# A two-layer graph network on one core: another order of the first and last stages, and their small operations on other engines

## The chip, the core and the metric

The kernel runs on one core of a Trainium2 chip. The core has a matrix engine (TensorE, PE in the profile), three engines for element-wise work (VectorE or DVE, ScalarE or ACT, GpSimd or POOL), and SyncE (SP), whose queue here issues nearly all transfers. Each engine works through its own list of instructions strictly in order; semaphores make one engine wait for another. The metric is the device time of one execution in microseconds (us); lower is better.

## What is computed

128 graphs, each with 128 nodes of 512 features (x) and a weighted adjacency matrix of 128x128 (adj). Everything is fp32.

```python
# layer 0
h = relu(layernorm(x))
# hypergraph conv, twice: H = (adj != 0), w = adj's first row
#   xw = x @ W.T ; m = Be * (H.T @ xw) ; out = Dn * (H @ m) + b
#   Dn = 1 / (H @ w), Be = 1 / column sums of H
h1 = layernorm(relu(hypergraph_conv(h, adj, W1, b1)), gamma, beta)   # 512 -> 1024
x = x + hypergraph_conv(h1, adj, W2, b2) + h                         # 1024 -> 512
# layer 1
h = relu(layernorm(x))
agg = (adj @ h) / max(rowsum(adj), 1e-6)
x = x + relu(concat([h, agg]) @ W.T)
```

gamma and beta of the inner layer norm are folded into the second weight matrix: its rows are scaled by gamma (scale_w2), and beta times it is a constant row (beta_row, summed on TensorE over eight parts, beta_out).

## The kernel before, in words

**Products in three parts.** TensorE multiplies fp32 at full precision slowly and a shorter format (fp32r) fast. So both factors of every large product are split in a high part h and a low part l, and a third combination d corrects the sum: product() (line 413) makes h times h and l times l in one PSUM bank (pm) and d times d in another (pd). The three weight matrices, each in two halves (w1, w2, w3, class Half), are split once at the start: high() on ScalarE, low() on VectorE, and rest(), which makes d, on VectorE or GpSimd (l - h, one instruction of 1024 columns) or, without an engine, on TensorE with a unit matrix and two ScalarE copies.

**One graph, in stages.** Each stage is a small function with the graph's number. x_sums, x_spread, scales, x_norm are the first layer norm; incidence (VectorE, from adjb, a copy of adj laid out in 32x32 blocks) and node_matrix make the 128x128 node operator S and Dn; conv1_nodes applies it, conv1_high/low/rest split the result, conv1_weights(g, half) multiplies with a half of w1; conv1_main (ScalarE) and conv1_out (VectorE) bring pm and pd into R, conv1_bias adds b1. inner_sums, inner_spread, inner_norm normalise R. For the transpose R goes to DRAM and comes back in blocks: inner_out, inner_in (four transfers), inner_turn; inner_high/low/rest split it, conv2_weights multiplies with w2, conv2_main, conv2_weights_out, conv2_bias give G, conv2_nodes and conv2_out add the result to x. residual (GpSimd) adds h and b2 to x. Layer 1 goes the same way: layer1_sums to layer1_norm, layer1_trip_out and layer1_trip_in through DRAM, layer1_turn, high, low, rest, then layer1_mean (the half of w3 for the mean, split again by layer1_mean_high/low/rest), layer1_self (the other half), aggregate with the transposed mean matrix (mean_operator, mean_out, mean_in, mean_transpose, mean_rest), layer1_self_main, layer1_self_out, finish with the store.

**The order is written out by hand.** Under manual_schedule the instructions of each engine stand in the order in which the stages are called. step(s) (line 694) is the steady loop; it works on the graphs from s - 4 to s + 3 at once. A stage that has been called for a graph is not done again (the set done, line 107), and calls for graphs that do not exist do nothing. So head() (line 761) may do stages of the first graphs early, and the loop leaves them out; tail() (line 986) does what the loop has left for the last five graphs, which it calls a to e (123 to 127). For the last graph tail() transposes on TensorE (layer1_now, turned_now, line 535) in place of the way through DRAM.

**Queues and buffers.** A stage's engine argument says where it runs: conv1_bias, conv2_bias, inner_low, layer1_low and layer1_mean_low run on GpSimd, in pieces of 256 columns, unless nc.vector is given. x_t has six buffers and adjb two, but R, G/H3 (tag A), H0 (tag B) and the landing tiles of the round trips have one, so that a stage can have to wait until the last reader of the graph before is through. PSUM has six banks for products (w) and two for node products (n).

**Fillers.** fill(columns) puts matmuls of a constant (line 94) ahead of the next product, into its bank; their result is overwritten. head() has ten of them and tail() three, 9600 columns in all.

Of the kernel before, what the change touches and what calls it, by code (L numbers as in the profile page):

```python
# [24 lines left out]
def gnn_kernel(  # L25
# [31 lines left out]
    nc = tc.nc  # L57
# [305 lines left out]
    @stage  # L363
    def x_spread(g):
        spread((1, g), X[g], H0[g], D)
# [395 lines left out]
    def head():  # L761
        copy(eps_root, eps, AF.Sqrt)
        load_x(0)
        load_adjb(2)
        for half in range(2):
            for i in range(2):
                load_w1(half, i)
        load_affine()
        unit()
        load_adjb(0, nc.scalar)  # L770
        load_adjb(1)
        load_x(1)
        x_sums(0)
        load_adj(0)
        x_spread(0)
        scales(0, 1)
        for half in range(2):
            load_w2(half)
        load_bias(b2_bc, b2)
        x_norm(0)  # L780
        w1[0].high(0)
        w1[0].high(1)
        load_x(2)
        incidence(0)
        w1[0].low(0)
        fill(2944)
        node_matrix(0)
        conv1_nodes(0)
        w1[0].low(1)
        w1[1].high(0)  # L790
        conv1_high(0)
        w1[1].high(1)
        w1[0].rest(0, nc.vector)
        load_bias(b1_bc, b1)
        conv1_low(0)
        conv1_rest(0)
        x_sums(1, "A")
        x_spread(1)
        node_scale(0)
        w1[0].rest(1, nc.vector)  # L800
        scales(1, 1)
        w1[1].low(1)
        fill(512)
        x_norm(1)
        incidence(1)
        w1[1].low(0)
        conv1_weights(0, 0)
        conv1_main(0, 0)
        beta_row(0)
        scale_w2(0, nc.scalar)  # L810
        node_matrix(1)
        beta_row(1)
        scale_w2(1, nc.scalar)
        w1[1].rest(0, nc.vector)
        w1[1].rest(1, nc.vector)
        w2[0].high(0)
        conv1_nodes(1)
        conv1_high(1, True)
        conv1_weights(0, 1)
        conv1_low(1)  # L820
        conv1_rest(1)
        beta_row(2)
        beta_row(3)
        conv1_main(0, 1)
        conv1_out(0, 0)
        scale_w2(2, nc.vector)
        load_adjb(3)
        scale_w2(3, nc.vector)
        conv1_weights(1, 0)
        conv1_bias(0, 0, nc.vector)  # L830
        w2[0].high(1)
        conv1_out(0, 1)
        conv1_bias(0, 1, nc.vector)
        beta_row(4)
        load_w3(1)
        load_w3(0)
        beta_row(5)
        beta_row(6)
        node_scale(1)
        residual(0)  # L840
        beta_row(7)
        inner_sums(0)
        conv1_weights(1, 1)
        w2[0].low(1)
        inner_spread(0)
        scale_w2(5, nc.vector)
        scale_w2(4, nc.vector)
        scales(0, 2)
        scale_w2(6, nc.vector)
        x_sums(2)  # L850
        scale_w2(7, nc.vector)
        w2[0].low(0)
        incidence(2)
        fill(256)
        inner_norm(0)
        inner_out(0)
        x_spread(2)
        scales(2, 1)
        w2[1].high(0)
        w2[1].low(0)  # L860
        node_matrix(2)
        x_norm(2)
        node_scale(2)
        w2[1].high(1)
        load_adjb(4)
        fill(384)
        conv1_nodes(2)
        conv1_main(1, 0)
        conv1_main(1, 1)
        conv1_high(2)  # L870
        w2[0].rest(1)
        conv1_low(2)
        conv1_rest(2)
        beta_out()
        inner_in(0)
        inner_turn(0)
        residual(1)
        conv1_out(1, 0)
        w3[0].high(0)
        fill(512)  # L880
        load_x(3)
        conv1_out(1, 1)
        w2[1].low(1)
        load_x(4)
        conv1_bias(1, 0, nc.vector)
        inner_high(0)
        conv1_weights(2, 0)
        conv1_bias(1, 1, nc.vector)
        conv1_weights(2, 1)
        inner_low(0, nc.vector)  # L890
        w2[0].rest(0)
        inner_sums(1)
        inner_spread(1)
        x_sums(3)
# [273 lines left out]
```

## Time and profile before

| | |
|---|---|
| three runs | 2497.18, 2497.54, 2499.67 us (median 2497.54) |
| span of the profiled execution, first to last instruction | 2496.5 us |
| mean granted clock of TensorE | 0.999 |
| TensorE, share of the span busy | 99% |
| DMA, share of its 16 engines busy, mean of the 40 slices 1 / 2 / 20 / 40 | 0.6 / 0.3 / 0.4 / 0.2 |
| first matmul of the kernel's own work | 9.23 us |
| last matmul starts | 2491.05 us |
| longest waits of TensorE up to 110 us | third part nd 2.8 (two times), w2 by DMA 2.5, G 1.8 (two times) |

How to read the lines that follow: a row of the timeline gives start, length, engine, line, operation, output<-inputs, shape and count, and in brackets how long the engine was idle before it and what it waited for. Names are those of the program with buffer numbers left out: ps_s is a node matrix's bank, pz and py are node products, rm/rd the two banks of conv1_weights, gm/gd of conv2_weights, bm/bd of layer1_mean, am/ad of layer1_self, pc the beta row. L94 is a filler. A group's length is from the start of its first to the modelled end of its last instruction; because matmuls are pipelined, the distance between two starts is the better measure of work. Rows of windows give start:end, length, busy time of each engine with its number of instructions, the granted clock, the share of the DMA engines that was busy, and GB/s.

### The profile page before, as it was taken

To read this page: it belongs to the slowest core of one execution; us is meant where nothing else is said; L and a number is where in the kernel's file an instruction comes from. 1 tells how busy PE (TensorE), PEld (TensorE's weight loads), DVE (VectorE), ACT (ScalarE), POOL (GpSimd) and SP (SyncE) were. 2 spreads that over 40 slices of the span, in tenths; PEclk is the share of its full clock that TensorE was granted. 3 is DMA by queue.
4 is the path that set the end of the run, shared out by engine and by line. 5 is a ranking of instruction groups with operands and counts; after the bars stand their busy time and mean duration, and the time that the engine had idled before them with its cause. 6 is when DMAs were issued, how large, how long until landed. Compare 5 with 4: busy or idle time off the path is not lost.

```text
span 2496.5 us, 41112 instructions
## 1 busy us (share of the span) xinstructions
PE 2473.9 (99%) x11220; PEld 2008.3 (80%) x11220; DVE 2003.6 (80%) x4913; ACT 1941.1 (78%) x4122; POOL 1701.1 (68%) x2269
## 2 busy tenths in 40 slices
PE   8999999999999999999999999999999999999998
PEld 5688888888888888888888888888888888888886
DVE  7888887888888788888888888888888888888886
ACT  6788778778877877887787788778778877877784
POOL 2476777677667767776776777677677767767770
PEclk9999999999999999999999999999999999999999
DMA  6333443443344344334434433443443344344432
GB/s 176 108 121 120 131 125 120 128 132 121 118 132 126 120 128 131 120 119 126 133 120 128 130 119 121 129 130 120 128 128 122 120 128 132 121 125 130 122 113 87
DMA packets 408951, 311.35 MB, mean 125 GB/s; under 512 B 176656, under 2 KB 339984, under 8 KB 408720
## 3 DMA queue, kind: packets, MB, share of 16 engines
q1 hardware_dynamic: 407888, 308.66, 40.2%
q8 instruction: 88, 1.44, 0.3%
q14 instruction: 143, 1.17, 0.2%
q10 hardware_dynamic: 576, 0.07, 0.0%
q0 software_dynamic: 256, 0.01, 0.0%
HBM read 166.21 MB, written 142.34 MB: 124 GB/s over the span
## 4 chain that ended last, share of the span: by engine, by line
PE 96%; ACT 1%; DVE 1%; DMA 1%; issue 0%; SPq 0%; POOL 0%; DVEq 0%; ACTq 0%
PE rm L422 18%; PE gm L422 18%; PE bm L422 9%; PE rd L427 9%; PE gd L427 9%; PE am L422 9%; PE bd L427 5%; PE ad L427 5%; PE pz L380 4%; PE py L595 4%; PE am L677 2%; PE ad L677 1%; PE ps_s L342 1%; DMA w11r<-in_w1t_dram 0%; ACT junk L266 0%
## 5 line engine op out<-in xcount | busy, mean ns | idle before, releaser
L80 POOL TENSOR_TENSOR g<-g,c 128x256 f32<-128x256 f32 x248 | 178.6, 743 | 634.4 <-DVE g L586 634.4
L80 POOL TENSOR_TENSOR r<-r,b_bc 128x256 f32<-128x256 f32 x496 | 358.1, 743 | 46.4 <-DVE r L447 36.0
L80 POOL TENSOR_TENSOR nl<-nt,nh 128x256 fp32r<-128x256 f32 x500 | 354.6, 741 | 30.3 <-ACT nh L504 30.3
L80 POOL TENSOR_TENSOR x_t<-x_t,b_bc 128x256 f32<-128x256 f32 x256 | 240.6, 959 | 15.3 <-DMA b_bc<-in_b_dram 15.3
L261 ACT ACTIVATE h<-x_t 128x512 f32<-128x512 f32 x256 | 160.0, 625 | 105.3 <-DVE x_t L599 102.9
L671 ACT ACTIVATE o<-am 128x512 f32<-128x512 f32 x128 | 76.5, 598 | 207.4 <-PE am L677 207.4
L80 POOL TENSOR_TENSOR hl<-ht,hh 128x256 fp32r<-128x256 f32 x248 | 231.7, 955 | 2.3 <-ACT hh L504 2.2
L80 POOL TENSOR_TENSOR x_t<-x_t,h 128x256 f32<-128x256 f32 x256 | 181.2, 726 | 45.0 <-ACT h L277 45.0
L277 ACT ACTIVATE h<-x_t,st 128x512 f32<-128x512 f32 x255 | 205.0, 804 | 1.4 <-DVE st L273 1.3
L447 DVE SCALAR_TENSOR_TENSOR r<-rd,dinv,r 128x512 f32<-128x512 f32 x256 | 190.6, 745 | 17.2 <-PE rd L427 2.9
L650 DVE TENSOR_TENSOR gb_t<-bd,gb_t 128x512 f32<-128x512 f32 x128 | 88.6, 692 | 140.4 <-ACT gb_t L646 136.7
L599 DVE SCALAR_TENSOR_TENSOR x_t<-py,dinv,x_t 128x512 f32<-128x512 f32 x128 | 96.1, 750 | 118.5 <-PE py L595 118.5
L266 ACT ACTIVATE h<-x_t,st 128x512 f32<-128x512 f32 x256 | 183.7, 717 | 4.3
L380 PEld LDWEIGHTS pz<-s,h 128*128 128x128 f32 x1024 | 134.3, 192 | 63.5 <-ACT s L344 42.9
L80 POOL TENSOR_TENSOR bl<-gb_t,bh 128x256 fp32r<-128x256 f32 x248 | 179.1, 745 | 0.0
L442 ACT ACTIVATE r<-rm,dinv 128x512 f32<-128x512 f32 x256 | 173.3, 677 | 1.2 <-PE rm L422 1.2
L586 DVE TENSOR_TENSOR g<-gd,g 128x512 f32<-128x512 f32 x128 | 88.5, 692 | 94.6 <-PE gd L427 89.2
L483 DVE STREAM_TRANSPOSE nt<-nb 128x1024 f32<-128x1024 f32 x128 | 157.7, 1232 | 3.8 <-DMA nb<-n_scratch 3.7
L277 ACT ACTIVATE r<-r,st 128x1024 f32<-128x1024 f32 x128 | 157.8, 1233 | 0.9 <-DVE st L273 0.9
L688 DVE SCALAR_TENSOR_TENSOR o<-o,x_t 128x512 f32<-128x512 f32 x128 | 154.5, 1207 | 4.2
L513 DVE SCALAR_TENSOR_TENSOR nd<-nh,nl 128x1024 fp32r<-128x1024 f32 x128 | 155.9, 1218 | 0.0
L422 PE MATMUL rm<-w11h,z 128*128 128x512 f32 x512 | 151.4, 417 | 0.0
(161 smaller groups left out, 7228.2 us busy)
## 6 DMA issues: line engine op xcount, KB each, us to landing
n_scratch<-r SPq DMA_DIRECT2D x128, 512.0 KB, 2.7
nb<-n_scratch SPq DMA_DIRECT2D x512, 128.0 KB, 2.8
x_t<-in_x_dram SPq DMA_DIRECT2D x128, 256.0 KB, 3.1
out_dram<-o SPq DMA_DIRECT2D x128, 256.0 KB, 2.3
h_scratch<-h SPq DMA_DIRECT2D x127, 256.0 KB, 2.0
hb<-h_scratch SPq DMA_DIRECT2D x508, 64.0 KB, 2.0
adj_t<-in_adj_dram SPq DMA_DIRECT2D x128, 64.0 KB, 1.9
an_scratch<-adj_t SPq DMA_DIRECT2D x128, 64.0 KB, 1.7
```

Source lines behind the costliest of these rows:

```text
L80: eng.tensor_tensor(dst[:, s], a[:, s], b[:, s], op)
L261: copy(junk, src, func, accum_out=t[:, 0:1])
L266: copy(junk, src, AF.Square, bias=t[:, 1:2], accum_out=t[:, 2:3])
L277: copy(dst, src, func, bias=t[:, 5:6], scale=t[:, 4:5])
L380: nc.tensor.matmul(z[:, k * P : (k + 1) * P], H0[g][:, k * P : (k + 1) * P], S[g], start=True, stop=True)
L422: nc.tensor.matmul(pm, left[i](k), right(i, k), start=(i == 0 and k == 0), stop=(i == 1 and k == kk - 1))
L427: nc.tensor.matmul(pd, left[2](k), right(2, k), start=(k == 0), stop=(k == kk - 1), skip_group_check=True)
L442: copy(R[g][:, HALVES[half]], PY.pop((g, half)), AF.Copy, scale=DN[g][:, 1:2])
L447: nc.vector.scalar_tensor_tensor(r, PR.pop((g, half)), dn[:, 0:1], r, MUL, ADD)
L483: nc.vector.transpose(nt.rearrange("p k (i b) -> p k i b", b=B), t.rearrange("p i k a -> p k i a"))
L513: nc.vector.scalar_tensor_tensor(t, h, 2.0**-12, low, MUL, SUB)
L688: nc.vector.scalar_tensor_tensor(o, o, 0.0, X.pop(g), MAX, ADD)
```

## The change

head() and tail() get another order; step() and all stages stay as they are. The same stages are done for the same graphs in head() and tail(), with the same number of matmuls on TensorE apart from the fillers. Besides the order:

- fillers: of ten in head() two of 640 columns each remain; the three in tail() are gone; together 1280 columns in place of 9600
- third parts: w1[0].rest(0), w2[1].rest(1) and w3[0].rest(0) go from VectorE to GpSimd; of the five on TensorE w3[1].rest(0), w3[1].rest(1), w3[0].rest(1) and both of w2[0] stay
- bias of conv1: (0, 0), (1, 0), (1, 1), (2, 0), (2, 1) and (127, 0) go from VectorE to GpSimd
- scalings of w2: parts 0, 1, 2, 5, 6 on ScalarE, 3 and 4 on GpSimd, 7 on VectorE (before: 0 and 1 on ScalarE, the rest on VectorE)
- low parts: layer1_low(0), layer1_low(125), layer1_mean_low(124) and (125) from VectorE to GpSimd, inner_low(127) from GpSimd to VectorE
- loads: x(1) and x(0) come first, adjb(0) on ScalarE's queue ahead of its first instruction, b2 and b1 ahead of the second half of w2, adjb(2), adj(0) and w3 later
- graph 1's first sums come ahead of graph 0's, and the square root of eps behind both

The diff, with the old bodies (printed above) cut:

```diff
     def head():
...
+        load_x(1)
+        load_adjb(0, nc.scalar)
+        x_sums(1, "A")
+        load_x(0)
+        x_sums(0)
+        copy(eps_root, eps, AF.Sqrt)
+        load_adjb(1)
+        load_w1(0, 0)
+        x_spread(1)
+        x_spread(0)
+        load_w1(0, 1)
+        incidence(0)
+        node_matrix(0)
+        unit()
+        scales(1, 1)
+        fill(640)
+        scales(0, 1)
+        load_w1(1, 0)
+        load_w1(1, 1)
+        incidence(1)
+        load_w2(0)
+        w1[0].high(0)
+        x_norm(0)
+        w1[0].high(1)
+        load_x(2)
+        load_bias(b2_bc, b2)
+        conv1_nodes(0)
+        node_matrix(1)
+        w1[0].low(0)
+        conv1_high(0)
+        load_affine()
+        load_bias(b1_bc, b1)
+        w1[1].high(0)
+        w1[0].low(1)
+        w1[0].rest(1, nc.vector)
+        w1[1].high(1)
+        node_scale(0)
+        conv1_low(0)
+        x_norm(1)
+        w1[0].rest(0, nc.gpsimd)
+        conv1_rest(0)
+        w1[1].low(1)
+        fill(640)
+        conv1_weights(0, 0)
+        load_w2(1)
+        conv1_nodes(1)
+        beta_row(0)
+        w1[1].low(0)
+        w1[1].rest(1, nc.vector)
+        w1[1].rest(0, nc.vector)
+        load_adjb(2)
+        conv1_main(0, 0)
+        beta_row(1)
+        x_sums(2)
+        conv1_high(1, True)
+        scale_w2(0, nc.scalar)
+        conv1_low(1)
+        conv1_weights(0, 1)
+        beta_row(2)
+        conv1_out(0, 0)
+        scale_w2(1, nc.scalar)
+        conv1_main(0, 1)
+        beta_row(3)
+        x_spread(2)
+        w2[0].high(0)
+        conv1_rest(1)
+        conv1_weights(1, 0)
+        conv1_out(0, 1)
+        beta_row(4)
+        residual(0)
+        conv1_bias(0, 0)
+        conv1_bias(0, 1, nc.vector)
+        inner_sums(0)
+        scale_w2(3, nc.gpsimd)
+        inner_spread(0)
+        scales(0, 2)
+        scale_w2(2, nc.scalar)
+        scale_w2(4, nc.gpsimd)
+        beta_row(5)
+        inner_norm(0)
+        load_w3(0)
+        incidence(2)
+        beta_row(6)
+        w2[0].high(1)
+        node_scale(1)
+        scale_w2(5, nc.scalar)
+        w2[1].high(0)
+        beta_row(7)
+        node_matrix(2)
+        w2[0].low(1)
+        scales(2, 1)
+        inner_out(0)
+        conv1_weights(1, 1)
+        x_norm(2)
+        scale_w2(6, nc.scalar)
+        w2[0].low(0)
+        scale_w2(7, nc.vector)
+        load_adjb(3)
+        load_x(3)
+        beta_out()
+        conv1_main(1, 0)
+        conv1_out(1, 0)
+        conv1_nodes(2)
+        conv1_main(1, 1)
+        conv1_out(1, 1)
+        w2[1].high(1)
+        conv1_high(2)
+        incidence(3)
+        conv1_low(2)
+        conv1_rest(2)
+        inner_in(0)
+        residual(2)
+        x_sums(3)
+        inner_turn(0)
+        w2[1].low(0)
+        w2[1].low(1)
+        conv1_bias(1, 0)
+        conv1_bias(1, 1)
+        w2[0].rest(0)
+        w2[0].rest(1)
+        inner_sums(1)
+        load_w3(1)
+        residual(1)
+        inner_spread(1)
+        load_adj(0)
+        conv1_weights(2, 0)
+        load_adjb(5)
+        scales(1, 2)
+        conv1_weights(2, 1)
+        node_scale(2)
+        w2[1].rest(1, nc.gpsimd)
+        inner_high(0)
+        inner_low(0, nc.vector)
+        x_spread(3)
+        scales(3, 1)
+        node_matrix(3)
+        inner_rest(0)
+        w2[1].rest(0, nc.vector)
+        conv2_weights(0)
+        inner_norm(1)
+        inner_out(1)
+        load_x(4)
+        w3[0].high(0)
+        w3[1].high(0)
+        x_norm(3)
+        load_x(5)
+        conv2_main(0)
+        mean_operator(0)
+        w3[1].high(1)
+        conv1_nodes(3)
+        conv1_main(2, 0)
+        mean_out(0)
+        conv2_weights_out(0)
+        conv1_high(3, True)
+        w3[0].high(1)
+        conv2_bias(0, nc.vector)
+        conv1_out(2, 0)
+        conv1_main(2, 1)
+        residual(3)
+        conv1_low(3)
+        inner_in(1)
+        conv2_nodes(0)
+        conv2_out(0)
+        layer1_sums(0)
+        load_adjb(4)
+        conv1_rest(3)
+        conv1_out(2, 1)
+        layer1_spread(0)
+        conv1_bias(2, 0)
+        w3[0].low(1)
+        scales(0, 3)
+        inner_turn(1)
+        x_sums(4)
+        conv1_weights(3, 0)
+        conv1_weights(3, 1)
+        w3[1].low(0)
+        conv1_bias(2, 1)
+        layer1_norm(0)
+        inner_high(1)
+        layer1_trip_out(0)
+        inner_low(1, nc.vector)
+        inner_sums(2)
+        inner_spread(2)
+        inner_rest(1)
+        mean_in(0)
+        conv2_weights(1)
+        scales(2, 2)
+        inner_norm(2)
+        conv2_main(1)
+        w3[0].low(0)
+        layer1_trip_in(0)
+        w3[1].low(1)
+        conv2_weights_out(1)
+        layer1_turn(0)
+        x_spread(4)
+        w3[0].rest(1)
+        inner_out(2)
+        conv2_bias(1, nc.vector)
+        inner_in(2)
+        layer1_high(0)
+        w3[0].rest(0, nc.gpsimd)
+        load_adj(1)
+        layer1_low(0)
+        scales(4, 1)
+        w3[1].rest(1)
+        conv2_nodes(1)
+        x_norm(4)
+        node_scale(3)
+        w3[1].rest(0)
+        mean_transpose(0)
+        incidence(4)
+        load_adjb(6)
+        conv2_out(1)
+        node_matrix(4)
+        layer1_rest(0)
+        node_scale(4)
 
     def tail():
         a, b, c, d, e = range(N - 5, N)
...
+        layer1_high(b)
+        turn_unit()
+        layer1_self_main(a)
+        conv2_bias(c, nc.vector)
+        mean_out(b)
+        conv1_main(e, 0)
+        inner_out(d)
+        mean_in(b)
+        conv2_nodes(c)
+        conv1_weights(e, 1)
+        layer1_low(b, nc.vector)
+        layer1_self_out(a)
+        layer1_rest(b)
+        conv2_out(c)
+        conv1_out(e, 0)
+        layer1_sums(c)
+        inner_in(d)
+        layer1_spread(c)
+        finish(a)
+        layer1_mean(b)
+        conv1_main(e, 1)
+        mean_transpose(b)
+        scales(c, 3)
+        inner_turn(d)
+        conv1_out(e, 1)
+        layer1_norm(c)
+        conv1_bias(e, 0)
+        layer1_mean_main(b)
+        conv1_bias(e, 1, nc.vector)
+        load_adj(c)
+        inner_high(d)
+        layer1_mean_out(b)
+        inner_sums(e)
+        layer1_mean_high(b)
+        inner_low(d, nc.vector)
+        inner_spread(e)
+        layer1_mean_low(b)
+        layer1_self(b)
+        mean_operator(c)
+        scales(e, 2)
+        layer1_trip_out(c)
+        mean_out(c)
+        inner_norm(e)
+        layer1_trip_in(c)
+        inner_rest(d)
+        conv2_weights(d)
+        inner_out(e)
+        layer1_mean_rest(b)
+        conv2_main(d)
+        mean_rest(b)
+        aggregate(b)
+        load_adj(d)
+        conv2_weights_out(d)
+        conv2_bias(d, nc.vector)
+        layer1_self_main(b)
+        layer1_turn(c)
+        mean_in(c)
+        inner_in(e)
+        conv2_nodes(d)
+        conv2_out(d)
+        mean_operator(d)
+        mean_out(d)
+        layer1_high(c)
+        layer1_sums(d)
+        layer1_spread(d)
+        layer1_low(c)
+        layer1_rest(c)
+        layer1_mean(c)
+        scales(d, 3)
+        layer1_norm(d)
+        mean_transpose(c)
+        mean_in(d)
+        layer1_self(c)
+        inner_turn(e)
+        load_adj(e)
+        layer1_mean_main(c)
+        layer1_mean_out(c)
+        layer1_trip_out(d)
+        inner_high(e)
+        inner_low(e, nc.vector)
+        layer1_self_out(b)
+        inner_rest(e)
+        mean_rest(c)
+        layer1_mean_high(c)
+        layer1_mean_low(c)
+        layer1_trip_in(d)
+        conv2_weights(e)
+        layer1_mean_rest(c)
+        aggregate(c)
+        conv2_main(e)
+        finish(b)
+        conv2_weights_out(e)
+        conv2_bias(e)
+        layer1_turn(d)
+        layer1_high(d)
+        conv2_nodes(e)
+        layer1_self_main(c)
+        mean_operator(e)
+        mean_transpose(d)
+        conv2_out(e)
+        layer1_low(d)
+        layer1_rest(d)
+        mean_out(e)
+        layer1_sums(e)
+        layer1_self_out(c)
+        layer1_mean(d)
+        layer1_mean_main(d)
+        finish(c)
+        layer1_mean_out(d)
+        layer1_spread(e)
+        layer1_mean_high(d)
+        mean_rest(d)
+        mean_in(e)
+        scales(e, 3)
+        layer1_mean_low(d, nc.vector)
+        layer1_mean_rest(d)
+        layer1_self(d)
+        layer1_norm_now(e)
+        layer1_now(e)
+        layer1_rest(e)
+        aggregate(d)
+        layer1_self_main(d)
+        layer1_mean(e)
+        layer1_self_out(d)
+        layer1_mean_main(e)
+        mean_transpose(e)
+        layer1_self(e)
+        finish(d)
+        layer1_mean_out(e)
+        layer1_mean_high(e)
+        mean_rest(e)
+        layer1_mean_low(e, nc.vector)
+        layer1_mean_rest(e)
+        aggregate(e)
+        layer1_self_main(e)
+        layer1_self_out(e)
+        finish(e)
```

## The prediction

> **What bounds the kernel now.** I read the page first: engine shares, the slices, the chain that ended last.
>
> ```profile
> PE 2473.9 (99%) x11220; PEld 2008.3 (80%) x11220; DVE 2003.6 (80%) x4913; ACT 1941.1 (78%) x4122; POOL 1701.1 (68%) x2269
> ...
> PE   8999999999999999999999999999999999999998
> ...
> PE 96%; ACT 1%; DVE 1%; DMA 1%; issue 0%; SPq 0%; POOL 0%; DVEq 0%; ACTq 0%
> ```
>
> TensorE is the bound, and only the first and last slices are not full. The change touches exactly these. So I asked for the stretches (columns: length, busy time of each engine, granted clock, DMA share, GB/s):
>
> ```profile
> 9.20:84.70 75.50, 64.01 (x246) 42.82 (x247) 62.57 (x129) 52.45 (x98) 14.20 (x18) 0.98 0.57 148
> 84.70:103.70 19.00, 17.29 (x82) 13.86 (x81) 14.43 (x34) 16.17 (x35) 11.07 (x16) 1.00 0.30 97
> 103.70:2399.70 2296.00, 2296.00 (x10508) 1880.63 (x10508) 1854.99 (x4593) 1810.66 (x3868) 1634.93 (x2173) 1.00 0.41 125
> ```
>
> From 103.7 to 2399.7 us TensorE never stops; a graph takes 19.0 us and nothing there is edited: 0 us to gain. What can be gained lies outside, and "busy" hides part of it, since fillers count as busy. I therefore count by pitch: four 128x512 fp32r matmuls start 0.907 us apart in the steady part, so one product half (12) is 2.72 us; an fp32 half-instruction of a filler or a beta row is 0.43. Head work from the first node_matrix to the first conv1_nodes of the loop: eight conv1 halves 21.8, two conv2_weights 10.9, eight beta rows 6.9, five third parts on TensorE 4.55, node matrices and node products 6.1: **50.2 us**. It takes 75.5, so 25.3 us are idle, filler or slow clock. Before it lie 9.2 us of start. The tail's work is 41.1 us and takes 51.1 (2440.4 to 2491.6): 10 us lost. After the last matmul 4.9 us remain (two DVE steps, the store).
>
> The timeline of TensorE shows what the losses are (start, length, engine, line, operands, idle before):
>
> ```profile
> 0.93 7.74 PE L94 MATMUL ps_s<-eps 128*128 128x512 f32 x12 [0.93 <-DVE eps L127]
> 9.23 0.49 PE L342 MATMUL ps_s<-sb,adjt 128*128 128x129 f32 x2 [0.55 <-DVE sb L336]
> ...
> 18.99 1.34 PE L223 MATMUL pc<-w20r,gb 128*128 128x512 f32 x2 [2.53 <-DMA w20r<-in_w2t_dram]
> ...
> 71.37 1.88 PE L94 MATMUL py<-eps 128*128 128x512 f32 x4
> 74.78 1.12 PE L595 MATMUL py<-g,s 128*128 128x512 f32 x2 [1.53 <-DVE g L80]
> ```
>
> A filler followed by idle time (71.37) was not the delay: the operand was late. Taking it out alone gives nothing.
>
> **Fillers.** 9600 columns become 1280, both left at the start. By rows only a few are on the path: 512 at 41.4, 256 at 56.1, 384 at 61.2 (about 1.3 us together) and the last, in the chain:
>
> ```profile
> 2479.50 0.81 ACT L567 ACTIVATE h<-x_t,st 128x512 f32<-128x512 f32 x1
> ...
> 2482.50 0.60 ACT L544 ACTIVATE hh<-pt 128x512 fp32r<-128x512 f32 x1 [0.72 <-PE pt L542]
> ```
>
> hh is ready at 2483.1, but the 1408 filler columns hold layer1_mean(127) until 2484.8: 1.6 us.
>
> A rule speaks against dropping them. The windows at 18 to 24 us:
>
> ```profile
> 18.00:20.00 2.00, 1.01 (x2) 0.49 (x3) 1.83 (x8) 0.08 (x1) 0.00 (x0) 0.93 1.06 220
> 20.00:22.00 2.00, 2.00 (x5) 1.11 (x4) 1.97 (x3) 0.89 (x2) 0.00 (x0) 0.50 1.06 226
> 22.00:24.00 2.00, 2.00 (x11) 1.69 (x10) 0.76 (x1) 1.46 (x2) 0.00 (x0) 0.72 1.04 278
> ```
>
> After 2.53 us idle the clock was 0.50: 2x(0.07+0.50+0.28) = 1.7 us of work lost. The Trainium skill ("TensorE: Matmul & The Clock Gate", part 1 and the closing table) puts it differently: cold until some 3.4 us of sustained work, cold again after an idle gap of about 3 us or more. By the rule the old 2.5 us gap is harmless; by the row it costs 1.7. I take the row: gaps must stay below 2.5 us. In the new order I find none above 1.5 after the first products, so one cold phase remains, at the start, where the 7.74 us of filler are gone: about 4 us at half clock, mostly while TensorE waits for operands anyway; 0.3 us on the path, at most 1.7.
>
> **The new start.** SP issues x(1), x(0), adjb(1), w1, then at once half of w2, x(2), b2, b1, the rest of w2; adjb(2), w3 and adj(0) go later. SP no longer stops for incidence(0) (before: idle from w11 at 6.1 to 7.97). DMA share is about 1 from 6 to 34 us, so I count megabytes: w2's first half stands behind 2.6 MB instead of 2.8, so it lands at about 18.6 (before 19.0); b2 at 21 (before 24.3), w2's second half at 26. adjb(0) still comes over ScalarE's queue, with the operand at about 7.6, and incidence(0) is first on DVE: node_matrix(0) at 9.2 as before. eps_root goes behind two sums; a second table load would cost 1.28 (the row of line 762), before ScalarE waits at 9.8 anyway: 0.
>
> Now by hand, rows added engine by engine. x_norm(0) is behind the node copy and w10.high(0): conv1_nodes(0) at 11.9 (before 10.3). DVE has incidence(1) 1.5, two lows and a rest at 1.15, node_scale 0.7 ahead of conv1_low(0): z.l at 16.5, so conv1_weights(0,0) ends at 18.6 instead of 16.5. **2 us worse here.** But conv1_nodes(1) follows, and beta_row(0) at 19.4 finds w2 landed: the 2.53 us stall and its cold phase are gone. conv1_weights(0,1), (1,0) and beta rows run without a wait to 31.7 (before 34.3).
>
> **Third parts.** w10.rest(0), w21.rest(1), w30.rest(0) go to GpSimd as one instruction of 1024 columns: four times the 743 ns row, 2.9 us; 3.8 at the 959 ns of its slow row. Needed 3.7, 5 and over 5 us after their lows: hidden, at worst 0.3 us for the first. DVE is relieved of 1.15 each. TensorE still makes five. load_affine's eight issues (0.55 each) now precede w10.rest(0) on GpSimd; they end near 6 us, that starts at 14: 0.
>
> **Biases.** conv1_bias(0,0), (1,·), (2,·) on GpSimd 1.44 each against 0.6 on DVE; queued behind residuals of 2.8. (1,1) ends at 39.6, inner_sums(1) comes up on ScalarE at 40.5: hidden by 0.9; if not, it delays h's way to conv2_weights one for one. layer1_low(0), layer1_mean_low(124) and (125) move the same way (1.44 against 0.69) and end 2 to 4 us before their matmuls. In the tail conv1_bias(127,0) runs beside DVE.
>
> **Scalings.** Five are on ScalarE (two before; 0.66 each), two on GpSimd (no row of a scaling there: 0.7 to 3 us; I take the 1.4 of two 743 ns adds), one stays on DVE. Slack on GpSimd is 3 us or more: 0.
>
> **Rest of the head.** incidence(2) waits on DVE behind scales(0,2), i.e. behind inner_spread(0), done 28.5: matrix ready 30.5, needed 31.7. On SP inner_out(0) waits for inner_norm(0) until 30.4 with adjb(3), x(3) and inner_in(0) behind it: adjb(3) lands near 36, wanted at 36.7, x(3) at 37.5; a late one costs its delay. R has one buffer, so conv1_main(1,0) at 34.7 waits for inner_out(0) to land (34.5 if the 2.7 us of its row stretches to 4 beside w3): 0 to 1 us. conv1_weights(1,1) ends 34.7 (before 37.0), conv1_nodes(2) 35.6 (40.1), both third parts and conv1 of graph 2 end 43.6 (48.8; waits 0.8), conv2_weights(0) 50.0 (56.1; nh at 44.4, wait 0.8), conv1_weights(3,0) 55.3 (64.6; wait 1.0 for g), (3,1) follows at once where before the filler and a 1.53 us wait stood, conv2_weights(1) 64.4 (wait 1.0 for nh), three third parts, conv2_nodes(1), node_matrix(4), conv1_nodes(4) at 70.7. Before: 84.7. That is 14 us; my sums leave out handing over between engines, some 0.25 us at a dozen places, so I book **11 us** (6 to 14). The first step's 1.7 us wait for nd stays.
>
> **Tail.** inner_norm(127) ends at 2452.7 in both orders, and its round trip is in the chain:
>
> ```profile
> 2452.79 4.95 DMA n_scratch<-r
> 2459.18 2.75 DMA nb<-n_scratch
> ```
>
> so conv2_weights(127) still starts near 2464.3; SP puts adj(126) and mean_in(125) ahead of inner_in, inside the 4.95. Then: inner_low on DVE instead of GpSimd (1.2 against 2.85) takes away the 0.23 wait; layer1_turn(126) leaves the spot ahead of conv2_nodes(127); GpSimd's bias comes to 2472.0 (before 2473.1). layer1_mean(126) 2472.9 (2474.5). layer1_norm_now(127) ends 2478.0 (before 2480.3) and its turn no longer stands behind aggregate(126): layer1_mean(127) at 2479.5 instead of 2484.8, 5.3 us. After that both run the same. layer1_low(125) on GpSimd costs 0.5 earlier, within the wait for the round trip. Booked **4 us** (1 to 6).
>
> Sum: 11 + 4 = 15 off the span of 2496.5: 2481.5; the runs' median is 1.0 above the span: **2482.5 us**.
>
> **Rivals.** (1) The round trips and first loads set the pace whatever the order: w2 late again (2.5 + 1.7), the tail giving only its filler (1.6), nh(0) late by another 2: gain about 6.5, 2491. For it: DMA share 1.0 up to 34 us, 4.95 in the chain; against: w2 has fewer bytes ahead, and 1.5 us of other matmuls. (2) Gaps only change place: gain under 5, 2496. For it: DVE and ScalarE have 62 and 52 us of work in the head's 75; against: my walk has the needed instructions ahead of the long waits. (3) Slower: without fillers TensorE stays at half clock through the head's many short waits. Half clock costs 0.5 us per us of work, so it needs 30 us of cold work to eat the 15; 40 us give 2502.5. Against: the 0.5 to 1.5 us gaps at 37 to 84 us left the clock at 1.00.
>
> Chances: forecast 0.64, (1) 0.21, (2) 0.08, (3) 0.07. 0.2% is 5.0 us, about what a measurement here tells from no change: faster 0.85, same 0.08, slower 0.07. Range: from 22 us off (head 14, tail 6, 2 for spread) to rival (1): 2475 to 2491.
>
> **Signs.** Right: no wait for w20r, clock 1.00 from 16 us on, conv1_nodes(4) near 73, (127)'s last products 4 us nearer their first node product. Wrong: 0.5 clock after 16 us, a GpSimd third part that matmuls wait for, the steady stretch not at 19.0 per graph.

## The result, and the profile after

| | before | changed |
|---|---|---|
| median of six runs each | 2498.22 us (2497.18 to 2499.67) | 2490.07 us (2489.83 to 2491.23) |
| ratio, with its 95% interval | | 0.9967 [0.9956, 0.9979] |
| span of the profiled execution | 2496.5 us | 2488.0 us |
| head: start to the first matmul of conv1_weights(4,0) | 99.28 | 90.28 (-9.00) |
| steady part: from there to conv2_nodes(125) | 2341.16 | 2346.10 (+4.94) |
| tail: from there to the start of the last matmul | 50.62 | 46.21 (-4.41) |

The change brings 8.1 us (8.5 in the span) where 15 were forecast. The last three rows come from looking up the same TensorE instruction in both traces. The tail gave what was booked, the head 2 us less than booked, and the part that nobody edited takes 4.9 us more. Executions of one and the same kernel lie up to 2.7 us apart here, and a trace shows one of them.

The page of the changed kernel (engine shares, TensorE's slices, the chain) hides all this: one first slice of 7 in place of 8, the rest as before.

```profile
PE 2463.6 (99%) x11184; PEld 2003.8 (81%) x11184; DVE 1995.7 (80%) x4896; ACT 1940.8 (78%) x4126; POOL 1728.8 (69%) x2290
...
PE   7999999999999999999999999999999999999998
...
PE 96%; DVE 1%; DMA 1%; ACT 1%; issue 0%; SPq 0%; POOL 0%; DVEq 0%; ACTq 0%; POOLq 0%
```

The stretches, cut at the events of the table (first row: node_matrix(0) to conv1_nodes(4)):

```profile
7.74:76.04 68.30, 59.83 (x234) 42.10 (x234) 60.79 (x114) 56.01 (x106) 39.84 (x37) 1.00 0.67 177
76.04:90.28 14.24, 14.22 (x60) 11.84 (x61) 11.65 (x31) 12.54 (x28) 7.38 (x11) 0.88 0.19 65
90.28:2436.37 2346.09, 2346.09 (x10714) 1917.48 (x10713) 1884.34 (x4672) 1841.85 (x3933) 1665.54 (x2216) 1.00 0.40 125
2436.37:2482.58 46.21, 42.93 (x179) 32.18 (x177) 36.08 (x72) 25.13 (x53) 10.52 (x12) 1.00 0.28 90
```

The third row is the trap. TensorE is busy for all of it, at full clock, with no wait, and yet it is 4.9 us longer for the same matmuls (before: 10715 records in 2341.16 us; one is missing here). Only the distance between starts shows it.

TensorE's timeline in the head, the rows that decide (length, operands, wait before):

```profile
17.92 1.20 PE L422 MATMUL rm<-w10l,z 128*128 128x512 f32 x4 [1.40 <-DVE z L397]
...
20.76 1.88 PE L223 MATMUL pc<-w20r,gb 128*128 128x512 f32 x4
...
50.26 1.20 PE L422 MATMUL gm<-w20l,nl 128*128 128x512 f32 x4 [2.19 <-DVE nl L80]
...
75.23 0.46 PE L342 MATMUL ps_s<-sb,adjt 128*128 128x129 f32 x2 [1.35 <-DVE sb L336]
76.06 1.54 PE L380 MATMUL pz<-s,h 128*128 128x128 f32 x8 [0.37 <-ACT s L344]
77.25 2.05 PE L422 MATMUL bm<-w30h,hh 128*128 128x512 f32 x4
```

The first beta row (20.76) no longer waits for w2: the 2.53 us stall of before is gone. In its place stand 1.40 and 2.19 us for low parts from VectorE, and a late 1.35 with slow matmuls behind it. What VectorE and GpSimd did before the first of these:

```profile
13.58 1.23 DVE L156 TENSOR_TENSOR w10d<-w10l,w10h 128x1024 fp32r<-128x1024 f32 x1
...
14.90 0.16 DVE L353 RECIPROCAL inv<-inv 128x1 f32<-128x1 f32 x1
15.10 1.95 DVE L355 SCALAR_TENSOR_TENSOR dinv<-s,inv 128x1 f32<-128x1 f32 x1
17.09 0.15 DVE L356 TENSOR_SCALAR dinv<-dinv 128x1 f32<-128x1 f32 x1
```

```profile
13.63 3.40 POOL L156 TENSOR_TENSOR w10d<-w10l,w10h 128x1024 fp32r<-128x1024 f32 x1 [7.40 <-DVE w10l L148]
```

An operation on one element per partition takes 1.95 us and ends at 17.05, with GpSimd's third part (17.03). conv1_low(0) stands behind it, and TensorE behind that. The same happens at 46.83: dinv takes 2.06 us and ends at 48.89, with GpSimd's third part w21d (48.86).

### The profile page after: what moved, and what is told of

Read it like the earlier page. It is cut to its first block, busy times and chain, and to the rows that moved or that the text cites. A ratio compares the mean times of both kernels' runs of the same rounds, so it can differ in the third digit from the quotient of the medians.

```text
span 2488.0 us, 41088 instructions
## 1 busy us (share of the span) xinstructions
PE 2463.6 (99%) x11184; PEld 2003.8 (81%) x11184; DVE 1995.7 (80%) x4896; ACT 1940.8 (78%) x4126; POOL 1728.8 (69%) x2290
## 4 chain that ended last, share of the span: by engine, by line
PE 96%; DVE 1%; DMA 1%; ACT 1%; issue 0%; SPq 0%; POOL 0%; DVEq 0%; ACTq 0%; POOLq 0%
PE rm L422 18%; PE gm L422 18%; PE bm L422 9%; PE am L422 9%; PE gd L427 9%; PE rd L427 9%; PE bd L427 5%; PE ad L427 5%; PE pz L380 4%; PE py L595 4%; PE am L677 2%; PE ad L677 1%; PE ps_s L342 1%; DMA b_bc<-in_b_dram 0%; DMA adjb<-in_adj_dram 0%
## 5 line engine op out<-in xcount | busy, mean ns | idle before, releaser
L80 POOL TENSOR_TENSOR r<-r,b_bc 128x256 f32<-128x256 f32 x508 | 366.9, 744 | 60.0 <-DVE r L447 51.7
```

The source lines that it names most:

```text
L80: eng.tensor_tensor(dst[:, s], a[:, s], b[:, s], op)
```

## The experiments

All segments below are cut as in the table above; a step is the distance from one aggregate to the next, averaged over 110 steps. Medians are over all executions; head, steady part, tail and step are those of the one execution that was traced.

| kernel | median us | ratio to before [95%] | head | steady | tail | step |
|---|---|---|---|---|---|---|
| changed | 2490.07 | 0.9967 [0.9956, 0.9979] | 90.28 | 2346.10 | 46.21 | 19.052 |
| 1 before's addresses | 2485.07 | 0.9949 [0.9932, 0.9965] | 90.49 | 2341.16 | 46.18 | 19.012 |
| 2 before, changed's addresses | 2503.75 | 1.0023 [1.0014, 1.0031] | 99.35 | 2346.10 | 50.81 | 19.052 |
| 3 thirds on VectorE | 2490.77 | 0.9971 [0.9960, 0.9982] | 90.47 | 2346.12 | 46.18 | 19.052 |
| 4 thirds in pieces | 2489.07 | 0.9963 [0.9950, 0.9976] | 89.37 | 2346.10 | 46.21 | 19.052 |
| 5 anp alone moved | 2489.25 | 0.9967 [0.9955, 0.9979] | 90.28 | 2345.27 | 46.21 | 19.045 |
| 6 before, no head fillers | 2497.38 | 0.9997 [0.9989, 1.0006] | 100.55 | 2341.16 | 48.40 | 19.012 |
| 7 warm start | 2491.01 | 0.9972 [0.9962, 0.9982] | 92.51 | 2346.10 | 46.24 | 19.052 |
| 8 all three | 2483.08 | 0.9940 [0.9928, 0.9953] | 88.32 | 2341.16 | 46.21 | 19.012 |
| 9 R alone moved | 2490.12 | 0.9970 [0.9958, 0.9982] | 90.55 | 2346.10 | 46.19 | 19.052 |
| 10 all but R moved | 2485.56 | 0.9953 [0.9938, 0.9968] | 90.23 | 2341.16 | 46.18 | 19.012 |
| 11 before, changed's tail | 2494.41 | 0.9984 [0.9978, 0.9991] | 99.99 | 2341.16 | 46.20 | 19.012 |
| 12 all and node_matrix(4) | 2484.85 | 0.9945 [0.9933, 0.9958] | 89.81 | 2341.56 | 46.22 | 19.012 |

### The steady part: where the small buffers lie (1, 2, 5, 9, 10)

The instruction lists of a step are the same in both kernels. Two things differ: the phase in which transfers and the other engines run beside TensorE, and the SBUF addresses of the small buffers, which the pool hands out in the order of their first use, so in the order of head(). The first experiment asks for the buffers in the old order ahead of head(), without writing to them:

```diff
+    for tag, shape, kind, bufs in (
+        ("x", [128, 512], mybir.dt.float32, 6),
+        ("adjb", [128, 128], mybir.dt.float32, 2),
+        ("anp", [P, 3, P], mybir.dt.float32, 1),
+        ("ant", [128, 128], mybir.dt.float32, 1),
...
+    ):
+        for _ in range(bufs):
+            pool.tile(shape, kind, tag=tag, name=tag + "_first", bufs=bufs)
+
     with tc.manual_schedule():
         head()
```

> The changed kernel, with its small SBUF buffers put at the addresses that they have in the kernel before (they are handed out in the order of first use, which the new head changes); no instruction is added or taken away. Theory (addresses): eight matmuls around aggregate that start 3 to 9 ns later than before in every step go back to 226.7 ns, a step from 19.05 to 19.01 us, and 123 steps give 4.9 us: 2485.2 us. Rival (the steps run in another phase with the transfers and the other engines): a step stays at 19.05 and the time at 2490.

The second does the reverse with the kernel before:

> The kernel before, with its small SBUF buffers at the addresses of the changed kernel. Theory (addresses): a step goes from 19.01 to 19.05 us, 2503 us. Rival (phase): a step stays at 19.01, 2498 us.

Both came out as the theory of the addresses has it: 2485.07 and 2503.75, steady 2341.16 and 2346.10. TensorE around one aggregate, the changed kernel and then the one with the old addresses:

```profile
1022.19 1.08 PE L427 MATMUL gd<-w21d,nd 128*128 128x512 f32 x4
1023.11 0.39 PE L677 MATMUL am<-bh,anp 128*128 128x512 f32 x1
...
1023.80 1.09 PE L422 MATMUL rm<-w10h,z 128*128 128x512 f32 x4
1024.73 1.07 PE L422 MATMUL rm<-w10l,z 128*128 128x512 f32 x4
```

```profile
1020.47 1.07 PE L427 MATMUL gd<-w21d,nd 128*128 128x512 f32 x4
1021.37 0.39 PE L677 MATMUL am<-bh,anp 128*128 128x512 f32 x1
...
1022.05 1.07 PE L422 MATMUL rm<-w10h,z 128*128 128x512 f32 x4
1022.96 1.07 PE L422 MATMUL rm<-w10l,z 128*128 128x512 f32 x4
```

From gd<-w21d to the first rm<-w10l it is 2.54 us in the one and 2.49 in the other, with no wait in brackets anywhere. In ns from one start to the next, means over 110 steps (bh, bl, bd are aggregate's three matmuls, rm 1 to 4 those of the first rm<-w10h):

```
                          last gd  am bh  am bl  ad bd  rm 1   rm 2   rm 3   rm 4
before, 1, 10              226.7   226.7  226.7  226.7  226.7  226.7  226.7  226.7
changed, 2, 9              235.0   230.8  229.2  230.8  235.8  228.4  232.5  230.8
5 (anp alone)              225.8   235.8  230.8  235.9  228.3  232.5  230.8  226.7
```

Which buffer? anp, aggregate's weights, begins at a multiple of 64 bytes in the kernel before; in the changed kernel it begins at a multiple of 32 but not of 64. One edit asks for it ahead of ht, which puts it back on a multiple of 64:

> The changed kernel with one buffer asked for earlier: anp, the three parts of the mean matrix that aggregate's matmuls load as weights, comes to 214336 (a multiple of 64 bytes, as in the kernel before) from 217632 (a multiple of 32 only). ht, sb, cnt and s move up by 1536 bytes and keep their remainder by 64; every other buffer stays where it is. Theory (it is anp's start that slows the eight matmuls around aggregate): a step goes from 19.05 to 19.01 us, total 2485.2. Rival (another buffer, G/H3, adj or ant, whose remainder also changed, or two buffers against each other): a step stays at 19.05, total 2490.

The excess falls from 40 to 33 ns and lies on six matmuls in place of eight: where anp lies has a part in it, but it isn't the cause, and the theory fell. The next suspect was R, whose transfer to DRAM runs at 410 GB/s through the first of these matmuls. Asking for adj ahead of R moves R and junk to their old places (and adj itself, which the expectation leaves out); the counterpart takes the old order with adj behind junk:

> The changed kernel with only R and the tile behind it (junk, o) at the addresses of the kernel before (R 220448 in place of 219936); anp, G/H3, H0, the matrix tiles and the landing tiles stay at the changed kernel's. Theory (the transfer of R to DRAM, which runs at 410 GB/s from 1.4 us before to 0.4 us after aggregate's last matmul, meets TensorE's reads only where R lies): a step 19.01 us, total 2485.2. Rival (another buffer): a step 19.05, 2490.

> The counterpart: the changed kernel with anp, ant, B, G/H3 and the landing tiles at or within 512 bytes of the addresses of the kernel before and with the same remainder by 64, but R and junk/o left at the changed kernel's 219936 and 224096. Theory (R's place decides): a step 19.05 us, total 2490. Rival (one of the others): 19.01, 2485.2.

R is cleared: moved without the others it changes nothing, and with the others at or near their old places the step is 19.012. Its transfer is also over before the slow matmuls are: from 1023.7 to 1024.7 us of the changed kernel the DMA engines move nothing, and rm 1 to 4 are slow there. That addresses make the 4.9 us is shown, by both directions; which buffer does it, alone or together with another, stays open.

### VectorE held up by GpSimd (3, 4)

The third parts back on VectorE:

```diff
-        w1[0].rest(0, nc.gpsimd)
+        w1[0].rest(0, nc.vector)
...
-        w2[1].rest(1, nc.gpsimd)
+        w2[1].rest(1, nc.vector)
...
-        w3[0].rest(0, nc.gpsimd)
+        w3[0].rest(0, nc.vector)
```

> The changed kernel with the third parts of w1[0] (first half), w2[1] (second half) and w3[0] (first half) back on VectorE. Theory (a long GpSimd instruction holds up VectorE until its end): the one-element dinv operations of node_scale(0) and node_scale(2) go from 1.95 and 2.06 us to under 0.3, TensorE's wait of 1.40 us for z's low part goes below 0.4, that of 2.19 for nl to about 1.2 (VectorE now has 1.15 of its own ahead of it): 2 us or so less, head ends (first half of conv1_weights of graph 4) at 88.3 in place of 90.3, total 2488. Rival (the slow dinv has another cause, or VectorE is the bound there): the three times 1.15 us on VectorE come on top, head the same or up to 2 us later, 2490 to 2492.

The mechanism is right, the gain absent. First VectorE, then TensorE of this kernel:

```profile
16.04 0.16 DVE L355 SCALAR_TENSOR_TENSOR dinv<-s,inv 128x1 f32<-128x1 f32 x1
```

```profile
17.05 1.19 PE L422 MATMUL rm<-w10l,z 128*128 128x512 f32 x4 [0.77 <-DVE z L397]
...
49.78 1.19 PE L422 MATMUL gm<-w20l,nl 128*128 128x512 f32 x4 [1.43 <-DVE nl L80]
...
75.49 0.46 PE L342 MATMUL ps_s<-sb,adjt 128*128 128x129 f32 x2 [2.19 <-DVE sb L336]
```

dinv is back at 0.16, the wait for z's low part is 0.77, that for nl 1.43. But w3[0]'s third part now stands on VectorE (1.22) ahead of incidence(4), and TensorE's wait for the sb that this one makes grows from 1.35 to 2.19: the head ends where it did. The other cure leaves GpSimd the work, in pieces of 256 columns:

```diff
             if eng:
+                if eng is nc.gpsimd:
+                    for k in (2 * i, 2 * i + 1):
+                        combine(eng, self.d[:, k], self.l[:, k], self.h[:, k], SUB)
+                    return
                 c = slice(2 * i, 2 * i + 2)
```

> The changed kernel with the three third parts left on GpSimd, each in four pieces of 256 columns instead of one of 1024. Theory (VectorE is held up until the end of the GpSimd instruction that runs): the dinv operations take at most one piece (0.75 to 0.95 us) and the waits of 1.40 and 2.19 us fall by 1 us each: head ends at 88.3, total 2488. Rival (what matters is GpSimd's work, not the length of one instruction): every VectorE operation waits for a piece, the sum stays, 2490.

VectorE and GpSimd of this kernel:

```profile
15.10 0.31 DVE L359 SCALAR_TENSOR_TENSOR dinv<-s,inv 128x1 f32<-128x1 f32 x1
```

```profile
13.63 4.90 POOL L80 TENSOR_TENSOR w10d<-w10l,w10h 128x256 fp32r<-128x256 f32 x4 [7.36 <-DVE w10l L148]
```

dinv takes 0.31 now, and GpSimd is the one that pays: 4.90 us for what took 3.40 in one piece. The wait for nl falls to 1.02, that for z's low part is gone, but TensorE waits 0.88 for the third part itself. 0.9 us of the head are left of it, half of what was expected.

### Fillers and the clock (6, 7)

The kernel before without its head's fillers, and the changed kernel with a filler more at the start:

```diff
-        fill(2944)
...
-        fill(384)
```

> The kernel before without the ten fillers of its head (7040 columns), its order unchanged; the three of the tail stay. Prediction's view: about 1.3 us of the head's fillers are on the path, and a colder start costs 0.3 (at most 1.7): 2497 to 2498.5. Rival (the fillers' own time was most of the head's loss): 4 us or more gone, 2494. Rival (they kept the clock up): half clock over the head's waits, 2503 or more.

```diff
         incidence(0)
+        fill(2304)
         node_matrix(0)
```

> The changed kernel with a filler of 2304 columns ahead of its first node matrix, to end about when that can start (7.7 us). Prediction's view (the cold start costs 0.3 on the path): first products at full pace (a node product 1.16 in place of 2.08 us), but the first conv1_weights waits for z's parts as before, time within 0.5 us of 2490. Rival (the cold start cost up to 1.7): 2488.5. Rival (the filler itself holds up the node matrix): up to 2 us more, 2492.

Taking the fillers out makes a difference that can't be told from none. The head is 1.3 longer (two runs of one and the same head, before and experiment 11, differ by 0.7), and the unedited tail 2.2 shorter: R's last transfer to DRAM landed 2.62 us after its issue here and 4.95 after it in the kernel before, so SP issues the way back at 2456.82 in place of 2457.87, although this tail begins 1.26 later. The waits for nh (0.67), nd (0.23) and hh (0.33) that followed it fall away, with the slower matmuls behind each. So this tail takes 48.40 or 50.62 us, depending on when one transfer lands. The head's 9 us come from its order and its choice of engines; the fillers taken away would not give them by themselves.

Four of the eight executions of the warm start took 2489.6 to 2490.1 us, hardly less than the changed kernel (2489.8 to 2490.3 in five of six); the other four took 2491.9 to 2492.3, outside the half microsecond expected. The traced one is of the latter, and its head is 2.2 longer. Its TensorE and windows:

```profile
17.89 2.08 PE L422 MATMUL rm<-w10l,z 128*128 128x512 f32 x4 [3.28 <-DVE z L397]
```

```profile
16.00:18.00 2.00, 0.11 (x1) 0.11 (x1) 1.97 (x4) 0.00 (x0) 2.00 (x3) 0.89 1.06 199
18.00:20.00 2.00, 2.00 (x5) 1.62 (x6) 2.00 (x3) 0.00 (x0) 0.44 (x2) 0.50 1.04 392
```

The first products ran at full pace (1.16 us for eight node products, 2.08 in the changed kernel), but the low part of z was there no sooner: rm<-w10l starts at 17.89 against 17.92. TensorE waited 3.28 us for it in place of 1.40, and in this execution the clock was low there instead, where the products behind it wait for nothing else. In the changed kernel the slow first matmuls lie in time that is waited through anyway.

### The late gap, and a better kernel (8, 12)

After the 1.35 us wait for sb the changed kernel's clock is low for over 3 us:

```profile
74.00:76.00 2.00, 0.46 (x2) 0.30 (x2) 1.93 (x5) 1.01 (x5) 2.00 (x4) 1.00 0.35 68
76.00:78.00 2.00, 1.95 (x10) 1.85 (x11) 1.90 (x6) 1.94 (x6) 0.36 (x1) 0.67 0.00 0
78.00:80.00 2.00, 2.00 (x7) 1.52 (x6) 1.97 (x5) 1.97 (x6) 1.43 (x2) 0.50 0.00 0
```

At clocks of 0.67 and 0.50 in these two windows, 2x(0.33+0.50) = 1.7 us of work are lost. One kernel takes the old addresses, the pieces, and this:

```diff
         conv2_bias(1, nc.vector)
+        incidence(4)
...
         mean_transpose(0)
-        incidence(4)
```

> The changed kernel with three things: the small buffers at the addresses of the kernel before, the three GpSimd third parts in pieces of 256 columns, and incidence(4) moved up on VectorE behind conv2_bias(1), ahead of the two scales and node_scale, so that node_matrix(4) no longer waits 1.35 us for sb. Theory: 4.9 (addresses) + 1.0 (pieces) + 1.3 (wait) + up to 1.7 (the half clock that follows this wait): 2481 to 2482.5. Rival (the late gap only moves on to the next operand, hl or hd of layer1_mean(0)): 2484.

2483.08 us, between the two: head -2.0, steady -4.9. The clock stays at 1.00. node_matrix(4) doesn't wait any more; conv1_nodes(4) waits 1.57 us. The row puts this down to hd, but it is the copy of s that ends last (74.68), behind two copies of w31d on ScalarE:

```profile
74.72 1.16 PE L384 MATMUL pz<-s,h 128*128 128x128 f32 x8 [1.57 <-DVE hd L517]
...
85.67 1.20 PE L431 MATMUL gd<-w20d,nd 128*128 128x512 f32 x4 [0.69 <-DVE nd L517]
```

The last kernel takes that away too (the edit is shown against experiment 8):

```diff
         incidence(4)
+        scales(4, 1)
...
-        scales(4, 1)
         w3[1].rest(1)
         conv2_nodes(1)
+        conv2_out(1)
...
         node_scale(3)
+        node_matrix(4)
         w3[1].rest(0)
...
-        conv2_out(1)
-        node_matrix(4)
```

> As the kernel with all three (addresses, pieces, incidence(4) earlier), and beyond it: node_matrix(4) ahead of the third part w3[1].rest(0) on TensorE and ScalarE, conv2_out(1) right behind conv2_nodes(1) on VectorE, scales(4,1) behind incidence(4). Theory (conv1_nodes(4) stood 1.57 us behind the copy of s, which was queued behind two copies of w31d on ScalarE, and behind the bank of py): it starts at 73.5 in place of 74.7, total 2481.9. Rival (the next operand, h or hh, is then late): 2483.

conv1_nodes(4) does start at 73.56 (74.72), but nothing is won: three of the five executions, the traced one among them, took 2484.9 to 2485.0 us, two took 2483.2 and 2483.5, and all five of experiment 8 took 2482.9 to 2483.1. TensorE of the traced one, and the windows there:

```profile
85.98 1.20 PE L431 MATMUL gd<-w20d,nd 128*128 128x512 f32 x4 [1.80 <-DVE nd L517]
...
89.81 1.47 PE L426 MATMUL rm<-w10h,z 128*128 128x512 f32 x4
```

```profile
86.00:88.00 2.00, 2.00 (x7) 1.67 (x8) 1.86 (x9) 1.55 (x5) 0.00 (x0) 0.81 0.56 147
88.00:90.00 2.00, 2.00 (x6) 1.52 (x6) 1.03 (x3) 0.37 (x1) 0.40 (x1) 0.50 0.63 262
```

nd, at the end of graph 2's round trip, is no earlier for it: TensorE starts on it at 85.98 after a wait of 1.80, in experiment 8 at 85.67 after 0.69. The time won is waited away there, and in this execution over 3 us at a low clock follow. That the two quicker executions were without them would fit their times, but no trace shows it. The kernel before waits for the same nd:

```profile
96.64 1.19 PE L427 MATMUL gd<-w20d,nd 128*128 128x512 f32 x4 [1.72 <-DVE nd L513]
```

### The tail alone (11)

> The kernel before with the changed kernel's tail alone. Theory (head, tail and addresses add up: 9.0, 4.4, minus 4.9): 4.4 us less than before, 2493.6, a step 19.01 us since the head is the old one, last matmul at 2486.7. Rival (the tail's gain needs the changed head's phase of transfers): 0 to 2 us less, 2496 to 2498.

The tail takes 46.20 in it, as in the changed kernel: it needs nothing of the new head, and in all eleven kernels that have this tail it is 46.18 to 46.24. The span (2492.8) is 3.7 less than before, since the head of this execution, unedited, ended 0.7 later; the median is 3.5 less. Nine of the twenty executions took 2492.6 to 2493.6, about what was expected, the others 2494.4 to 2495.1.

How much of the 4.4 us is the new order's own is less clear. In all eleven kernels R's last transfer lands 2.8 to 3.0 us after its issue. With the old tail it took 4.95 (before), 5.11 (experiment 2) and 2.62 (experiment 6), and with the 2.62 the old tail is only 2.2 us longer than the new one. Whether the new order makes the landing early was not tested.

## Why the prediction was right and wrong

**Sum.** 11 from the head and 4 from the tail were booked: 15. Measured: 9.0 + 4.4 - 4.9 = 8.5. The total still lies inside the range, 0.9 us from its upper end, and that is luck in part: this end stood for rival (1), late first loads and round trips, and not for what was lost. Two of the forecast's own signs of being wrong came true, clock 0.50 after 16 us and a step not quite at 19.0. Experiment 8, which takes away the three losses found, has a head of 88.32 and a span of 2481.1; the forecast implied 88.3 and 2481.5, so nearly all that is missing lies in three steps:

1. **"a graph takes 19.0 us and nothing there is edited: 0 us to gain".** This step failed, and it is 4.9 of the 6.5 us that are missing. 0.04 us a step doesn't show in a "19.0", but there are 123 steps. The head's order sets addresses, and addresses set the pitch of eight matmuls (experiments 1, 2 and 10).
2. **Third parts on GpSimd "hidden, at worst 0.3 us for the first".** The durations were fair (2.9 to 3.8 given; 3.40, 2.39 and 3.25 measured), and the matmuls that read these third parts didn't wait. What failed was to count only those: the one-element operations of node_scale(0) and (2) waited for GpSimd's end on VectorE, z and nl behind them, and TensorE 1.40 and 2.19. The prediction's own sign for this, "a GpSimd third part that matmuls wait for", was thought of in the wrong form. dinv has two SBUF inputs (s, inv) and took 1.95; the reciprocal just ahead of it has one and took 0.16 beside the same GpSimd instruction. A rule stood against the move and wasn't weighed: the Trainium skill ("GPSIMD Engine Reference", sections 1 and 8) says that GpSimd shares its SBUF interfaces with VectorE, with contention for VectorE instructions of two SBUF inputs. By the rows of durations alone the move was free; by the rule it had a price. Cutting the instruction up gives 0.9 us of it back. VectorE's own third part, also of two inputs, began 0.05 us ahead of GpSimd's (13.58, 13.63) and took its usual 1.23, while GpSimd's took 3.40, 1.0 more than the 2.39 of the second: it looks as if whichever starts first makes the other wait, which was not tested.
3. **"gaps must stay below 2.5 us. In the new order I find none above 1.5 ..., so one cold phase remains, at the start".** There are two, the second at 76 to 80 us. Neither the 2.5 us taken from the old row nor the 3 us of the skill's rule, which the prediction weighs, orders these traces: a wait of 1.35 (with 0.37 behind it) was followed by the 1.7 us loss, while one of 2.19 before 50.26 left the clock at 1.00. Little of it counted in the end: 1.35, 0.37 and 1.7 were lost there, but nd is late anyway, and the head of experiment 8 is only 1.05 shorter than that of experiment 4.

**Start.** "0.3 us on the path, at most 1.7" for the cold start was right, on the low side: the better half of the warm start's executions is some 0.2 us quicker than the changed kernel, which is within the spread. (The clock column reads 1.00 through this start; that it is slow shows in the 2.08 us of eight node products, 1.16 in the warm start.) node_matrix(0) and conv1_nodes(0) were even sooner (7.74 and 11.17; 9.2 and 11.9 forecast), and the first third part on GpSimd ate it: conv1_weights(0,0) ended at 19.9 in place of 18.6.

**w2.** "the 2.53 us stall and its cold phase are gone": right. So rival (1), first loads and round trips, fell in its mechanism, although the total lies near its 2491.

**Fillers.** About 1.3 us were seen on the path of the head. Taken out alone they gave nothing (experiment 6): as the prediction said of one of them, the operand was late. That holds for the 256 columns at 56.1 as well, which it counted: conv1_nodes(3) behind them waited 1.07 us for h.

**nd.** "The first step's 1.7 us wait for nd stays": it did not, because TensorE came there late, at 87.76. Experiment 12 brings it back as soon as TensorE is early.

**Tail.** Right in size, 4 booked and 4.4 measured, and in mechanism as far as it goes: layer1_norm_now(127) and the last products come forward as forecast. What it took as fixed is the 4.95 us of R's transfer, which took 2.85 here; with a quick transfer the old tail is 2.2 us shorter too (experiment 6). layer1_norm_now(127) was forecast to end at 2478.0; take off the 4.07 by which the tail starts earlier, and it is 2473.9. ScalarE and TensorE:

```profile
2473.34 0.81 ACT L567 ACTIVATE h<-x_t,st 128x512 f32<-128x512 f32 x1
...
2476.04 1.19 PE L422 MATMUL bm<-w30h,hh 128*128 128x512 f32 x4 [0.21 <-ACT hh L544]
```

It ends at 2474.15, and layer1_mean(127) follows 1.9 later where 1.5 was reckoned. The 2484.8 from which the forecast counted is the modelled end of the filler; the matmul's own row in the kernel before starts earlier, so by starts the fillers held it 1.2 us and not 1.6, and it came forward by 4.2 and not 5.3:

```profile
2484.33 1.38 PE L422 MATMUL bm<-w30h,hh 128*128 128x512 f32 x4
```

**Scalings and biases.** 1.4 us was guessed for a scaling on GpSimd; the two took 1.58 and 1.56, with no wait of TensorE behind them.

## What to carry to other kernels

When an edit changes the order in which buffers are first asked for, compare their addresses and the start-to-start distance in the part that was not edited: a busy share of 100% says nothing about 0.2%, and asking for the buffers in a fixed order up front keeps the addresses the same. Where executions of one kernel fall in two groups, as here in experiments 7 and 12, one trace is not enough to say what an edit costs. Before moving work to GpSimd, look at what VectorE does meanwhile, its smallest operations with two inputs above all, and try several short instructions in place of one long one. A wait taken away is worth only the distance to the next late operand: here 3.4 us were lost around the sb that was cured, and the cure gave 1.05, because nd was the next.

## What the runs showed of the hardware

- The pitch of 128x512 fp32r matmuls is 226.7 ns with one set of buffer addresses and up to 235.8 with another, for the same instructions and with no wait in the trace. What gets in the way was not found.
- A VectorE operation on 128x1 with two SBUF inputs that started during a GpSimd instruction of 1024 columns took 1.95 and 2.06 us, ending within 0.03 us of it, and 0.16 without it; with pieces of 256 columns it took 0.31 and 0.40.
- A 128x512 matmul in full fp32 is two instructions that start 0.43 us apart (conv2_nodes(125), 2436.37 and 2436.80); one in fp32r takes 0.227.
- The length of a gap doesn't decide about the clock. A wait of 2.19 us for nl before 50.26 left it at 1.00 in the changed kernel. In the warm-start kernel the same wait, one microsecond later, was followed by this window:

```profile
52.00:54.00 2.00, 2.00 (x6) 1.61 (x5) 2.00 (x2) 0.34 (x1) 1.58 (x2) 0.50 0.62 239
```

  Waits of 1.35 (sb, changed kernel) and 1.80 (nd, experiment 12) were followed by 0.50, waits of 1.57 (experiment 8) and 1.72 (before) were not. The Trainium skill ("TensorE: Matmul & The Clock Gate", part 1) speaks of a free-running activity window; that would make the place of a gap in it matter beside its length, which these rows and the two groups of executions of experiments 7 and 12 agree with but do not prove.
